# Two neighbouring rows on the partitions: six products in place of nine in the attention layer's output convolution

## The chip, the cores and the metric

The program runs on one core of one Trainium2 chip. TensorE does the matrix products into PSUM, VectorE (DVE) empties PSUM and does elementwise work and statistics, ScalarE (ACT) applies scale and bias, GpSimd (POOL) clears borders and copies, and SyncE's queue (SPq) issues nearly all the transfers, which run on 16 DMA engines. The metric is the time of one whole execution on the device, in microseconds. The kernel before takes 13737.34 us (median of 3 runs, 13731.92 to 13746.49).

## The reference, cut to what matters

Four layers, each `x = x + layer(group_norm(x))`, on four images of 48 channels and 256 x 256 pixels. The change concerns the first, an attention over channels:

```python
def _L0_conv_ref(x, qkv_w, dw_w, proj_w, temperature):
    qkv = conv1x1(x, qkv_w)                      # 48 -> 144 channels
    qkv = depthwise_conv3x3(qkv, dw_w)           # zero border
    q, k, v = split(qkv)                         # 48 channels each, over all 65536 pixels
    attn = softmax(einsum('bhcn,bhdn->bhcd', l2norm(q), l2norm(k)) * temperature)   # 48 x 48
    out = einsum('bhcd,bhdn->bhcn', attn, v)
    return conv1x1(out, proj_w)

x = x + _L0_conv_ref(_gn(x), ...)    # _gn: 16 groups of 3 channels, eps 1e-5
x = x + _L1_conv_ref(_gn(x), ...)    # next layer: needs the statistics of the new x
...
```

Once `attn` is known, projection, attention and the 1x1 convolution for `v` are three matrices on the channels of one image. Together with the depthwise 3x3 they make one 3x3 convolution of 48 to 48 channels whose weights differ from image to image.

## The kernel before: the parts that the change touches

`B, C, H, W = 4, 48, 256, 256`, `P = 96`, `R = 16` rows in a block, `NB = 16` blocks, `NP = 2` pairs of images. The 96 partitions hold two images of 48 channels each. First a pass over `x` gives the group norm's scale and bias for a pair (`coef[pair]`). Then for each pair: the products of q and k over all rows (`pqk`, `gram`), the softmax, the weights `wy`, and the output convolution (`py`), which reads `x` again.

```python
def ahead(items, load, work):            # loads of item i+1 stand before the work of item i
    ...

# layer 0: one block of 16 rows and its two neighbours, of both images of a pair
def load(pair, b):
    lo, hi = (1 if b == 0 else 0), (R + 1 if b == NB - 1 else R + 2)
    raw = raws.tile([P, R + 2, W], F32, tag="raw")                   # bufs=3
    src = x[rows(pair), (b * R - 1 + lo) * W : (b * R - 1 + hi) * W]
    nc.sync.dma_start(raw[:, lo:hi, :].rearrange(...), src)          # 18 KB in one piece per partition
    xn = big.tile([P, R + 2, W + 2], F32, tag="xn")                  # bufs=2
    nc.gpsimd.memset(...)                                            # borders
    nc.scalar.activation(xn[:, lo:hi, 1 : W + 1], raw[:, lo:hi, :], AF.Identity,
                         bias=coef[pair][:, 1:2], scale=coef[pair][:, 0:1])
    return raw, xn

# ... pqk and gram for all blocks, softmax, then pa = attention and projection of both images
wy = work.tile([P, 9, P], F32, tag="wy")
for t in range(9):
    wt = wv_sb * dwv_sb[:, t]                              # tensor_scalar_mul
    nc.tensor.matmul(pw, lhsT=wt, rhs=pa, start=True, stop=True)
    nc.vector.tensor_copy(wy[:, t, :], pw)                 # two 48 x 48 blocks, the rest zero

def outputs(b, loaded):
    raw, xn = loaded
    y = big.tile([P, R, W], F32, tag="y")
    for c in range(8):                                     # two rows of 256 in one PSUM bank
        ps = p_conv.tile([P, 2, W], F32, tag="pc", name="py")          # bufs=4
        for t, dy, dx in taps:                             # nine products
            nc.tensor.matmul(ps, lhsT=wy[:, t, :],
                             rhs=xn[:, 2 * c + dy : 2 * c + dy + 2, dx : dx + W],
                             start=t == 0, stop=t == 8)
        part = y[:, 2 * c : 2 * c + 2, :]
        nc.vector.tensor_add(part, ps, raw[:, 1 + 2 * c : 3 + 2 * c, :])
        nc.vector.bn_stats(stats[:, b * 8 + c, :], part)
    nc.sync.dma_start(x1[rows(pair), ...], y)              # 16 KB in one piece per partition

ahead(range(NB), lambda b: load(pair, b), outputs)
nc.vector.bn_aggr(mv, stats)
k.group_norm(work, p_small, mv, "mean3", coef1[pair])
```

The next layer starts with transfers of `x1` into tiles `tok`, which POOL copies into `pairs`, TensorE turns round (`ptok`) and DVE scales (`xt`) with `strip`, made from `coef1`.

Of the kernel before, what the change touches and what calls it, by code (L numbers as in the profile page):

```python
# [9 lines left out]
F32 = mybir.dt.float32  # L10
# [8 lines left out]
NP = 2  # L19
# [13 lines left out]
def _constants():  # L33
    i = np.arange(128)
    p = np.arange(P)
    group = lambda x: (x % C) // 3
    parts = {
        "ident": np.eye(128),

        "mean3": np.pad((p[:, None] // 3 == p[None] // 3) / 3.0, ((0, 32), (0, 0))),  # L40
        "mean6": np.pad((group(p)[:, None] == group(p)[None]) / 6.0, ((0, 32), (0, 0))),
        "mean8": (i[:, None] // F == i[None] // F) / float(F),
        "ones": np.ones((128, P)),

        "half": np.pad((p[:, None] // C == np.arange(2)[None]).astype(float), ((0, 32), (0, 0))),
        "diag48": np.pad((p[:, None] % C == np.arange(C)[None]).astype(float), ((0, 32), (0, 0))),

        "to_strip": np.pad(
            ((p[:, None] % 3 == 0) & (group(p)[:, None] % 2 == p[None] // C)).astype(float), ((0, 32), (0, 0))
        ),  # L50
        "of_strip": np.pad(
            (
                (p[:, None, None] // C == np.arange(2)[None, :, None])
                & (group(p)[:, None, None] // 2 == np.arange(G // 2)[None, None])
            ).reshape(P, G).astype(float),
            ((0, 32), (0, 0)),
        ),
    }
# [52 lines left out]
def rows(pair):  # L111
    return slice(pair * P, (pair + 1) * P)


@with_exitstack
def input_stats(ctx, tc, x, k, coef):

    nc = tc.nc
    big = ctx.enter_context(tc.tile_pool(name="s_big", bufs=4))
    work = ctx.enter_context(tc.tile_pool(name="s_work", bufs=2))  # L120
    psum = ctx.enter_context(tc.tile_pool(name="s_psum", bufs=2, space=PSUM))
    n = R * W

    def load(it):
        pair, b = it
        t = big.tile([P, n], F32, tag="x", name="sx")
        nc.sync.dma_start(t, x[rows(pair), b * n : (b + 1) * n])
        return t

    stats = [work.tile([P, NB * 8, 6], F32, tag="st", name=f"st{p}") for p in range(NP)]  # L130

    def add(it, t):
        pair, b = it
        for c in range(8):
            nc.vector.bn_stats(stats[pair][:, b * 8 + c, :], t[:, c * 512 : (c + 1) * 512])
        if b == NB - 1:
            mv = work.tile([P, 2], F32, tag="mv", name="mv")
            nc.vector.bn_aggr(mv, stats[pair].rearrange("p a b -> p (a b)"))
            k.group_norm(work, psum, mv, "mean3", coef[pair])

    ahead([(p, b) for p in range(NP) for b in range(NB)], load, add)


@with_exitstack
def layer0(ctx, tc, x, x1, wqk, dwqk, wv, dwv, projT, temp, k, coef, coef1):
# [18 lines left out]
    nc.sync.dma_start(wqk_sb, wqk)  # L164
    dw_sb = wp.tile([P, 9, NQ], F32, tag="dwqk", name="dw_sb")
    nc.gpsimd.dma_start(dw_sb.rearrange("p t o -> p (t o)"), dwqk.rearrange("t o -> (t o)").partition_broadcast(P))
    wq = wp.tile([P, 9, NQ], F32, tag="wq", name="wq")
    for t in range(9):
        nc.vector.tensor_mul(wq[:, t, :], dw_sb[:, t, :], wqk_sb)
# [9 lines left out]
    def load(pair, b):  # L179

        lo, hi = (1 if b == 0 else 0), (R + 1 if b == NB - 1 else R + 2)
        raw = raws.tile([P, R + 2, W], F32, tag="raw", name="raw")
        src = x[rows(pair), (b * R - 1 + lo) * W : (b * R - 1 + hi) * W]
        nc.sync.dma_start(raw[:, lo:hi, :].rearrange("p h w -> p (h w)"), src)
        xn = big.tile([P, R + 2, W + 2], F32, tag="xn", name="xn")
        nc.gpsimd.memset(xn[:, :, 0:1], 0.0)
        nc.gpsimd.memset(xn[:, :, W + 1 : W + 2], 0.0)
        if lo:
            nc.gpsimd.memset(xn[:, 0, :], 0.0)
        if hi < R + 2:  # L190
            nc.gpsimd.memset(xn[:, R + 1, :], 0.0)
        nc.scalar.activation(  # L192
            xn[:, lo:hi, 1 : W + 1], raw[:, lo:hi, :], AF.Identity, bias=coef[pair][:, 1:2], scale=coef[pair][:, 0:1]
        )
        return raw, xn

    taps = [(t, t // 3, t % 3) for t in range(9)]
    for pair in range(NP):
# [8 lines left out]
        pending = []  # L207

        def products(it, loaded):
            xn = loaded[1]  # L210
            for r in range(R):
                ps = p_conv.tile([128, 2, NQ], F32, tag="pc", name="pqk")
                for j in range(2):
                    for t, dy, dx in taps:
                        nc.tensor.matmul(  # L215
                            ps[:, j, :],
                            lhsT=xn[:, r + dy, dx + 128 * j : dx + 128 * j + 128],
                            rhs=wq[:, t, :],
                            start=t == 0,
                            stop=t == 8,  # L220
                        )
                qk = qkp.tile([128, 2, NQ], F32, tag="qk", name="qk")
# [18 lines left out]
            nc.tensor.matmul(pr, lhsT=k["ones", P], rhs=dg, start=True, stop=True)  # L241
            rsum.append(pr)
        norm = work.tile([P, P], F32, tag="norm", name="norm")
        half = k["half", P]
        nc.vector.tensor_scalar_mul(norm, rsum[0], half[:, 0:1])
        nc.vector.scalar_tensor_tensor(norm, rsum[1], half[:, 1:2], norm, ALU.mult, ALU.add)
        nc.vector.tensor_scalar_max(norm, norm, 1e-24)
# [24 lines left out]
        nc.tensor.matmul(pt, lhsT=attn.rearrange("p b d -> p (b d)"), rhs=proj_sb, start=True, stop=True)  # L272
        pa = work.tile([P, P], F32, tag="pa", name="pa")
        nc.vector.tensor_copy(pa, pt)
        wy = work.tile([P, 9, P], F32, tag="wy", name="wy")
        for t in range(9):
            wt = work.tile([P, P], F32, tag="wt", name="wt")
            nc.vector.tensor_scalar_mul(wt, wv_sb, dwv_sb[:, t : t + 1])
            pw = p_small.tile([P, P], F32, tag="small", name="pw")
            nc.tensor.matmul(pw, lhsT=wt, rhs=pa, start=True, stop=True)  # L280
            nc.vector.tensor_copy(wy[:, t, :], pw)

        stats = work.tile([P, NB * 8, 6], F32, tag="st", name="st")

        def outputs(b, loaded):
            raw, xn = loaded
            y = big.tile([P, R, W], F32, tag="y", name="y")
            for c in range(8):
                ps = p_conv.tile([P, 2, W], F32, tag="pc", name="py")
                for t, dy, dx in taps:  # L290
                    nc.tensor.matmul(  # L291
                        ps,
                        lhsT=wy[:, t, :],
                        rhs=xn[:, 2 * c + dy : 2 * c + dy + 2, dx : dx + W],
                        start=t == 0,
                        stop=t == 8,
                    )
                part = y[:, 2 * c : 2 * c + 2, :]
                nc.vector.tensor_add(part, ps, raw[:, 1 + 2 * c : 3 + 2 * c, :])  # L299
                nc.vector.bn_stats(stats[:, b * 8 + c, :], part.rearrange("p h w -> p (h w)"))  # L300
            nc.sync.dma_start(x1[rows(pair), b * R * W : (b + 1) * R * W], y.rearrange("p h w -> p (h w)"))

        ahead(range(NB), lambda b: load(pair, b), outputs)
        mv = work.tile([P, 2], F32, tag="mv", name="mv")
        nc.vector.bn_aggr(mv, stats.rearrange("p a b -> p (a b)"))
        k.group_norm(work, p_small, mv, "mean3", coef1[pair])


@with_exitstack
def layer1(ctx, tc, x1, x2, w1, w2, pw, cols, b2, k, coef1, coef2):  # L310
# [34 lines left out]

    strip = []
    for b in range(B):
        of = k["of_strip", P][:, (b % 2) * NS : (b % 2 + 1) * NS]
        one = wp.tile([P, 2, NS], F32, tag=f"strip{b}", name=f"strip{b}")
        for c in range(2):  # L350
            spread = work.tile([P, NS], F32, tag="spread", name="spread")
            nc.vector.tensor_scalar_mul(spread, of, coef1[b // 2][:, c : c + 1])
            ps = p_small.tile([P, NS], F32, tag="small", name="pstrip")
            nc.tensor.matmul(ps, lhsT=k["to_strip", P], rhs=spread, start=True, stop=True)
            nc.vector.tensor_copy(one[:, c, :], ps)
        strip.append(one)
# [474 lines left out]
def program(ctx, tc, a, out, at):  # L831
# [5 lines left out]
    coefs = [  # L837
        [const.tile([P, 2], F32, tag=f"coef{layer}_{p}", name=f"coef{layer}_{p}") for p in range(NP if layer < 2 else B)]
        for layer in range(4)
    ]  # L840
    x1 = dram.tile([B * C, HW], F32, tag="x1", name="x1")
# [19 lines left out]
def _layout(v):  # L861
# [4 lines left out]
    dw = v["L0_conv_dw_w"].reshape(3 * C, 9)  # L866
    a["wqk"] = _block_diag(qkv[: 2 * C].T, 2)
    a["dwqk"] = np.concatenate([dw[: 2 * C].T] * 2, 1)
    a["wv"] = _block_diag(qkv[2 * C :], 2)
# [63 lines left out]
```

## Time and profile before

| stretch of the span, us | what runs | TensorE busy, us |
|---|---|---|
| 0 to 240 | statistics of x | 4.16 |
| 240 to 1926 | pqk and gram, images 0 and 1 | 1681.05 |
| 1943 to 2928 | py, images 0 and 1 | 985.00 |
| 2935 to 4612 | pqk and gram, images 2 and 3 | 1677.00 |
| 4631 to 5617 | py, images 2 and 3 | 986.00 |
| 5617 to 7400 | second layer | 1273.20 |
| 7400 to 13280 | third and fourth layer | 5446.95 |
| 13280 to 13735 | output put in order | 0.00 |

How to read it: a stretch in which TensorE is busy from end to end gets shorter only if TensorE has less to do there; in the others something else ends the waits. "PE" is TensorE's products and "PEld" its weight loads, which go on beside the products. In this profile a product of 32-bit numbers appears as two instructions, so 2304 products of the output convolution are counted as x4608.

### The profile page before, as it was taken

Reading aid. Unit: us, or ns where it says so; the run is one execution under the profiler, and the core shown is the slowest. Engines: PE = TensorE matmul, PEld = TensorE weight load, DVE = VectorE, ACT = ScalarE, POOL = GpSimd, SP = SyncE. Lnnn points to the kernel's source line nnn. Section 1 sums busy time; section 2 is a strip of 40 time slices with the busy share of each in tenths; the row PEclk is TensorE's granted clock in tenths of the full one; section 3 lists DMA queues with packets and bytes.
Section 4 is the critical chain, followed back from the end, with each engine's and each line's share of the span. In section 5 each row is a group of like instructions: output and inputs, shape, how many; then the busy total and the mean of one; then the engine's idle time right before and its main releaser. Section 6 shows DMA issues by size and latency. Waiting matters only on the chain.

```text
span 13735.6 us, 130672 instructions
## 1 busy us (share of the span) xinstructions
PE 12080.9 (88%) x55056; PEld 8710.1 (63%) x55056; DVE 4075.2 (30%) x6994; ACT 3100.0 (23%) x4523; POOL 755.4 (5%) x367
## 2 busy tenths in 40 slices
PE   2999999999999999877866989899888989899960
PEld 2999973369999633333323767676665767676740
DVE  5000011110000111444543323354553323354530
ACT  0000000000000000111112533254444533354531
POOL 0000000000000000100100000000331000001430
PEclk9999999999999999988987999999998999999985
DMA  7000002110000021243326756664775756655889
GB/s 176 22 16 16 16 16 59 51 52 16 16 21 16 20 59 49 77 97 86 77 56 129 154 119 149 152 164 132 186 183 116 154 126 147 157 150 147 228 195 226
DMA packets 867508, 1383.31 MB, mean 101 GB/s; under 512 B 245064, under 2 KB 791016, under 8 KB 791560
## 3 DMA queue, kind: packets, MB, share of 16 engines
q1 hardware_dynamic: 866776, 1374.29, 42.1%
q8 instruction: 431, 7.06, 0.2%
q14 instruction: 157, 1.29, 0.0%
q0 software_dynamic: 144, 0.66, 0.0%
HBM read 820.20 MB, written 553.65 MB: 100 GB/s over the span
## 4 chain that ended last, share of the span: by engine, by line
PE 81%; SPq 5%; DMA 4%; issue 4%; DVE 3%; POOL 1%; ACT 1%; POOLq 0%; ACTq 0%; DVEq 0%
PE ps L564 35%; PE pqk L215 22%; PE py L291 14%; PE ph L386 3%; SPq L809 3%; PE gram L205 3%; PE psp L444 2%; DMA sx<-in_x 1%; SPq L504 1%; DMA xr<-x 1%; POOL sl L767 1%; PE pout L483 1%; DVE v L423 1%; PE ptok L391 1%; SPq L649 0%
## 5 line engine op out<-in xcount | busy, mean ns | idle before, releaser
L564 PE MATMUL ps<-carry,w_sb 96*96 96x256 f32 x24480 | 5443.1, 384 | 394.8 <-DVE carry L720 129.1
L564 PEld LDWEIGHTS ps<-carry,w_sb 96*96 96x96 f32 x24480 | 4030.8, 165 | 1806.4 <-DVE carry L566 170.2
L215 PE MATMUL pqk<-wq,xn 96*128 96x192 f32 x18432 | 3101.9, 327 | 12.4 <-ACT xn L192 10.9
L215 PEld LDWEIGHTS pqk<-wq,xn 96*128 96x128 f32 x18432 | 2991.4, 190 | 13.5 <-ACT xn L192 11.4
L291 PE MATMUL py<-xn,wy 96*96 96x512 f32 x4608 | 1985.3, 593 | 0.2
L568 DVE SCALAR_TENSOR_TENSOR carry<-ps,b_sb,col 96x256 f32<-96x256 f32 x2040 | 1359.6, 667 | 1247.0 <-PE ps L564 1215.6
L722 ACT COPY col<-carry 96x256 f32<-96x256 f32 x2040 | 1333.9, 654 | 1627.8 <-DVE carry L568 1627.8
L291 PEld LDWEIGHTS py<-xn,wy 96*96 96x96 f32 x4608 | 749.8, 163 | 1223.8 <-issue 1223.3
L192 ACT ACTIVATE xn<-raw,coef 96x4608 f32<-96x4608 f32 (+1 forms) x64 | 269.1, 4204 | 4990.0 <-PE pqk L215 3223.3
L223 DVE COPY qk<-pqk 128x384 f32<-128x384 f32 x512 | 285.5, 558 | 3083.0 <-PE pqk L215 3083.0
L767 POOL TENSOR_TENSOR sl<-sl,col 96x4096 f32<-96x4096 f32 x64 | 567.6, 8888 | 5314.3 <-ACT col L722 4514.6
L566 DVE TENSOR_TENSOR carry<-ps,up 96x256 f32<-96x256 f32 x1016 | 426.4, 421 | 1020.0 <-PE ps L564 921.1
L566 DVE TENSOR_TENSOR carry<-ps,dn 96x256 f32<-96x256 f32 x1020 | 427.7, 421 | 1000.0 <-PE ps L564 945.7
L299 DVE TENSOR_TENSOR y<-py,raw 96x512 f32<-96x512 f32 x256 | 175.8, 687 | 1611.6 <-PE py L291 1611.6
L623 ACT ACTIVATE dn<-carry,b_sb 96x256 f32<-96x256 f32 x1024 | 499.5, 504 | 660.8 <-DVE carry L566 660.5
L663 ACT COPY up<-carry 96x256 f32<-96x256 f32 x1016 | 410.0, 404 | 945.5 <-DVE carry L566 944.8
L483 PE MATMUL pout<-h,w_sb 128*96 128x512 f32 x512 | 341.0, 816 | 297.0 <-DVE y L491 296.2
L386 PE MATMUL ph<-xt,w_sb 96*128 96x512 f32 x1024 | 499.1, 608 | 103.7 <-DVE xt L393 81.1
L205 PE MATMUL gram<-qk 128*96 128x96 f32 x4096 | 431.3, 248 | 0.0
L483 PEld LDWEIGHTS pout<-h,w_sb 128*96 128x96 f32 x512 | 100.6, 216 | 520.9 <-issue 495.6
L205 PEld LDWEIGHTS gram<-qk 128*96 128x96 f32 x4096 | 428.6, 164 | 0.3
L393 DVE TENSOR_SCALAR xt<-ptok,strip 96x512 f32<-96x512 f32 x256 | 298.8, 1195 | 241.5 <-PE ptok L391 239.8
(108 smaller groups left out, 2950.4 us busy)
## 6 DMA issues: line engine op xcount, KB each, us to landing
dn<-x SPq DMA_DIRECT2D x256, 384.0 KB, 11.4
D<-dn SPq DMA_DIRECT2D x32, 3072.0 KB, 21.5
up<-D SPq DMA_DIRECT2D x32, 3072.0 KB, 28.2
col<-U SPq DMA_DIRECT2D x64, 1536.0 KB, 13.7
sl<-x SPq DMA_DIRECT2D x64, 1536.0 KB, 16.5
R<-col SPq DMA_DIRECT2D x64, 1536.0 KB, 11.7
col<-R SPq DMA_DIRECT2D x64, 1536.0 KB, 25.6
x<-sl SPq DMA_DIRECT2D x64, 1536.0 KB, 7.2
```

The costliest lines, as they stand in the source:

```text
L205: nc.tensor.matmul(grams[b], lhsT=part, rhs=part, start=first and j == 0, stop=last and j == 1)
L215: nc.tensor.matmul(ps[:, j, :], lhsT=xn[:, r + dy, dx + 128 * j : dx + 128 * j + 128], rhs=wq[:, t, :], start=t == 0, stop=t == 8,)
L291: nc.tensor.matmul(ps, lhsT=wy[:, t, :], rhs=xn[:, 2 * c + dy : 2 * c + dy + 2, dx : dx + W], start=t == 0, stop=t == 8,)
L386: nc.tensor.matmul(ph[f], lhsT=w1_sb[:, i, f, :], rhs=xt, start=i == 0, stop=i == NS - 1)
L483: nc.tensor.matmul(ps.rearrange("p h w -> p (h w)"), lhsT=w2_sb[:, i, :], rhs=h1[:, p0 : p0 + 512], start=True, stop=True,)
L564: nc.tensor.matmul(ps, lhsT=w_sb[:, way, j, :], rhs=old[:, :, j : j + W // 2], start=j == 0, stop=j == 2)
L566: nc.vector.tensor_add(blocks(new), blocks(ps), inp)
L568: nc.vector.scalar_tensor_tensor(new, ps, b_sb[:, way : way + 1], inp, ALU.add, ALU.add)
L623: nc.scalar.activation(inp, new, AF.Identity, bias=b_sb[:, 0:1])
L722: nc.scalar.copy(column, step(pair, way, column, False))
L767: nc.gpsimd.tensor_add(v, v, flat(got[pair]))
L809: nc.sync.dma_start(t[b * C : (b + 1) * C, r].rearrange("c k q h w -> c (k q) (h w)"), xin[r * C : (r + 1) * C, 2 * pair + b, :, n * NH : ...
```

## The change

The output convolution goes image by image. The 96 partitions hold the 48 channels of one image twice: an odd row below and the even row after it above (row -1 with row 0, row 1 with row 2, and so on). The outputs are rows 2m and 2m+1. They need the four rows 2m-1 to 2m+2, which are two such row pairs, so that two positions of the pair by three columns, six products, cover the 3x3 window of both output rows, where one row per partition needed nine. Each 96 x 96 weight matrix has three of its four 48 x 48 blocks filled. The aim is fewer products on TensorE for the same outputs.

With it come these: the rows are read and written with a step of two (pieces of 1 KB); the even rows are read once more for the residual, because `xn`'s order no longer matches the output's; the scale and bias are needed per image with both halves of the partitions alike, so the first pass over `x` goes per image, its two halves of the rows on the two halves of the partitions; the q and k products still go by pairs and put their scale and bias together from two images.

```diff
 # first pass: one image, upper and lower half of its rows on the two halves of the partitions
+        for half in range(2):
+            p0 = half * HW // 2 + i * n
+            nc.sync.dma_start(t[half * C : (half + 1) * C], x[b * C : (b + 1) * C, p0 : p0 + n])
-            k.group_norm(work, psum, mv, "mean3", coef[pair])
+            k.group_norm(work, psum, mv, "mean6", coef[b])
 ...
+    M = R // 2
+    def load_odd(b, n, edges):
+        t = big.tile([P, M + 1, W], F32, tag="odd", name="odd")          # bufs=2, like all of big
+        ...
+        for r in range(2):
+            lo, hi = ...
+            h0 = n * R - 1 + r
+            nc.sync.dma_start(t[r * C : (r + 1) * C, lo:hi, :], src[:, h0 + 2 * lo : h0 + 2 * hi - 1 : 2, :])
+        even = big.tile([P, M, W], F32, tag="even", name="even")
+        for r in range(2):
+            nc.sync.dma_start(even[r * C : (r + 1) * C], src[:, n * R + r : n * R + r + R - 1 : 2, :])
+        xn = big.tile([P, M + 1, W + 2], F32, tag="xodd", name="xodd")
+        nc.gpsimd.memset(...)                                            # borders
+        nc.scalar.activation(xn[:, lo:hi, 1 : W + 1], t[:, lo:hi, :], AF.Identity, bias=g[:, 1:2], scale=g[:, 0:1])
+        if edge is not None:                                             # first and last block: the row outside is zero
+            nc.scalar.activation(xn[:, edge, 1 : W + 1], t[:, edge, :], ...)
+        return xn, even
 ...
-            nc.vector.tensor_copy(wy[:, t, :], pw)
+            nc.vector.tensor_copy(py[:, t, :], pw)
+        for b in (2 * pair, 2 * pair + 1):
+            wy = work.tile([P, 2, 3, 2, C], F32, tag="wy", name="wy")
+            ...                                                          # six DVE instructions fill it from py
+            def outputs(n, loaded):
+                xn, even = loaded
+                y = big.tile([P, M, W], F32, tag="y", name="y")
+                for c in range(M // 2):
+                    ps = p_conv.tile([P, 2, W], F32, tag="pc", name="py")
+                    for i in range(6):
+                        j, dx = i // 3, i % 3
+                        nc.tensor.matmul(ps, lhsT=wy[:, j, dx].rearrange("p r o -> p (r o)"),
+                                         rhs=xn[:, 2 * c + j : 2 * c + j + 2, dx : dx + W],
+                                         start=i == 0, stop=i == 5)
+                    part = y[:, 2 * c : 2 * c + 2, :]
+                    nc.vector.tensor_add(part, ps, even[:, 2 * c : 2 * c + 2, :])
+                    nc.vector.bn_stats(stats[:, n * 4 + c, :], part.rearrange("p h w -> p (h w)"))
+                for r in range(2):
+                    nc.sync.dma_start(dst[:, n * R + r : n * R + r + R - 1 : 2, :], y[r * C : (r + 1) * C])
+            ahead(range(NB), lambda n: load_odd(b, n, edges), outputs)
+            ...
+            k.group_norm(work, p_small, mv, "mean6", coef1[b])
```

More of the change, by code (lines that the diff above doesn't have):

```diff
@@ L38, in _constants @@
         "ident": np.eye(128),
-        "mean3": np.pad((p[:, None] // 3 == p[None] // 3) / 3.0, ((0, 32), (0, 0))),
         "mean6": np.pad((group(p)[:, None] == group(p)[None]) / 6.0, ((0, 32), (0, 0))),
@@ L122, in input_stats @@
     n = R * W
+    nb = NB // 2
     def load(it):
-        pair, b = it
+        b, i = it
         t = big.tile([P, n], F32, tag="x", name="sx")
-        nc.sync.dma_start(t, x[rows(pair), b * n : (b + 1) * n])
+        for half in range(2):
+            p0 = half * HW // 2 + i * n
+            nc.sync.dma_start(t[half * C : (half + 1) * C], x[b * C : (b + 1) * C, p0 : p0 + n])
         return t
-    stats = [work.tile([P, NB * 8, 6], F32, tag="st", name=f"st{p}") for p in range(NP)]
+    stats = [work.tile([P, nb * 8, 6], F32, tag="st", name=f"st{b}", bufs=B) for b in range(B)]
     def add(it, t):
-        pair, b = it
+        b, i = it
         for c in range(8):
-            nc.vector.bn_stats(stats[pair][:, b * 8 + c, :], t[:, c * 512 : (c + 1) * 512])
-        if b == NB - 1:
+            nc.vector.bn_stats(stats[b][:, i * 8 + c, :], t[:, c * 512 : (c + 1) * 512])
+        if i == nb - 1:
             mv = work.tile([P, 2], F32, tag="mv", name="mv")
-            nc.vector.bn_aggr(mv, stats[pair].rearrange("p a b -> p (a b)"))
-            k.group_norm(work, psum, mv, "mean3", coef[pair])
-    ahead([(p, b) for p in range(NP) for b in range(NB)], load, add)
+            nc.vector.bn_aggr(mv, stats[b].rearrange("p a b -> p (a b)"))
+            k.group_norm(work, psum, mv, "mean6", coef[b])
+    ahead([(b, i) for b in range(B) for i in range(nb)], load, add)
 @with_exitstack
@@ L166, in layer0 @@
     nc.gpsimd.dma_start(dw_sb.rearrange("p t o -> p (t o)"), dwqk.rearrange("t o -> (t o)").partition_broadcast(P))
+    half = k["half", P]
+    pairs = []
+    for pair in range(NP):
+        both = wp.tile([P, 2], F32, tag=f"both{pair}", name=f"both{pair}")
+        nc.vector.tensor_scalar_mul(both, coef[2 * pair], half[:, 0:1])
+        nc.vector.scalar_tensor_tensor(both, coef[2 * pair + 1], half[:, 1:2], both, ALU.mult, ALU.add)
+        pairs.append(both)
     wq = wp.tile([P, 9, NQ], F32, tag="wq", name="wq")
@@ L192, in load @@
         nc.scalar.activation(
-            xn[:, lo:hi, 1 : W + 1], raw[:, lo:hi, :], AF.Identity, bias=coef[pair][:, 1:2], scale=coef[pair][:, 0:1]
+            xn[:, lo:hi, 1 : W + 1], raw[:, lo:hi, :], AF.Identity, bias=pairs[pair][:, 1:2], scale=pairs[pair][:, 0:1]
         )
-        return raw, xn
+        return xn
+    M = R // 2
+    def load_odd(b, n, edges):
+        t = big.tile([P, M + 1, W], F32, tag="odd", name="odd")
+        src = x[b * C : (b + 1) * C, :].rearrange("c (h w) -> c h w", w=W)
+        edge = 0 if n == 0 else M if n == NB - 1 else None
+        if edge is not None:
+            nc.gpsimd.memset(t[:, edge, :], 0.0)
+        for r in range(2):
+            lo, hi = (1 if edge == 0 and r == 0 else 0), (M if edge == M and r == 1 else M + 1)
+            h0 = n * R - 1 + r
[4 more added lines that the diff above has]
+        xn = big.tile([P, M + 1, W + 2], F32, tag="xodd", name="xodd")
+        nc.gpsimd.memset(xn[:, :, 0:1], 0.0)
+        nc.gpsimd.memset(xn[:, :, W + 1 : W + 2], 0.0)
+        g = coef[b]
+        lo, hi = (1 if edge == 0 else 0), (M if edge == M else M + 1)
+        nc.scalar.activation(
+            xn[:, lo:hi, 1 : W + 1], t[:, lo:hi, :], AF.Identity, bias=g[:, 1:2], scale=g[:, 0:1]
+        )
+        if edge is not None:
+            g = edges[edge == M]
+            nc.scalar.activation(
+                xn[:, edge, 1 : W + 1], t[:, edge, :], AF.Identity, bias=g[:, 1:2], scale=g[:, 0:1]
+            )
+        return xn, even
     taps = [(t, t // 3, t % 3) for t in range(9)]
@@ L209, in products @@
         def products(it, loaded):
-            xn = loaded[1]
+            xn = loaded
             for r in range(R):
@@ L243, in layer0 @@
         norm = work.tile([P, P], F32, tag="norm", name="norm")
-        half = k["half", P]
         nc.vector.tensor_scalar_mul(norm, rsum[0], half[:, 0:1])
@@ L274, in layer0 @@
         nc.vector.tensor_copy(pa, pt)
-        wy = work.tile([P, 9, P], F32, tag="wy", name="wy")
+        py = work.tile([P, 9, P], F32, tag="py", name="py")
         for t in range(9):
@@ L280, in layer0 @@
             nc.tensor.matmul(pw, lhsT=wt, rhs=pa, start=True, stop=True)
-            nc.vector.tensor_copy(wy[:, t, :], pw)
[L283 to L306, printed above, removed]
+            nc.vector.tensor_copy(py[:, t, :], pw)
+        for b in (2 * pair, 2 * pair + 1):
+            wy = work.tile([P, 2, 3, 2, C], F32, tag="wy", name="wy")
+            tap = lambda dy: py[:, 3 * dy : 3 * dy + 3, (b % 2) * C : (b % 2 + 1) * C]
+            nc.vector.tensor_scalar_mul(wy[:, 0, :, 0, :], tap(0), half[:, 0:1])
+            nc.vector.scalar_tensor_tensor(wy[:, 0, :, 0, :], tap(1), half[:, 1:2], wy[:, 0, :, 0, :], ALU.mult, ALU.add)
+            nc.vector.tensor_scalar_mul(wy[:, 0, :, 1, :], tap(0), half[:, 1:2])
+            nc.vector.tensor_scalar_mul(wy[:, 1, :, 0, :], tap(2), half[:, 0:1])
+            nc.vector.tensor_scalar_mul(wy[:, 1, :, 1, :], tap(1), half[:, 0:1])
+            nc.vector.scalar_tensor_tensor(wy[:, 1, :, 1, :], tap(2), half[:, 1:2], wy[:, 1, :, 1, :], ALU.mult, ALU.add)
+            edges = []
+            for r in (1, 0):
+                e = work.tile([P, 2], F32, tag=f"edge{r}", name=f"edge{r}")
+                nc.vector.tensor_scalar_mul(e, coef[b], half[:, r : r + 1])
+                edges.append(e)
+            stats = work.tile([P, NB * 4, 6], F32, tag="st", name="st")
+            def outputs(n, loaded):
[5 more added lines that the diff above has]
+                        j, dx = i // 3, i % 3
+                        nc.tensor.matmul(
+                            ps,
+                            lhsT=wy[:, j, dx].rearrange("p r o -> p (r o)"),
+                            rhs=xn[:, 2 * c + j : 2 * c + j + 2, dx : dx + W],
+                            start=i == 0,
+                            stop=i == 5,
+                        )
+                    part = y[:, 2 * c : 2 * c + 2, :]
+                    nc.vector.tensor_add(part, ps, even[:, 2 * c : 2 * c + 2, :])
+                    nc.vector.bn_stats(stats[:, n * 4 + c, :], part.rearrange("p h w -> p (h w)"))
+                dst = x1[b * C : (b + 1) * C, :].rearrange("c (h w) -> c h w", w=W)
+                for r in range(2):
+                    nc.sync.dma_start(dst[:, n * R + r : n * R + r + R - 1 : 2, :], y[r * C : (r + 1) * C])
+            ahead(range(NB), lambda n: load_odd(b, n, edges), outputs)
+            mv = work.tile([P, 2], F32, tag="mv", name="mv")
+            nc.vector.bn_aggr(mv, stats.rearrange("p a b -> p (a b)"))
+            k.group_norm(work, p_small, mv, "mean6", coef1[b])
@@ L347, in layer1 @@
     for b in range(B):
-        of = k["of_strip", P][:, (b % 2) * NS : (b % 2 + 1) * NS]
+        of = k["of_strip", P][:, :NS]
         one = wp.tile([P, 2, NS], F32, tag=f"strip{b}", name=f"strip{b}")
@@ L351, in layer1 @@
             spread = work.tile([P, NS], F32, tag="spread", name="spread")
-            nc.vector.tensor_scalar_mul(spread, of, coef1[b // 2][:, c : c + 1])
+            nc.vector.tensor_scalar_mul(spread, of, coef1[b][:, c : c + 1])
             ps = p_small.tile([P, NS], F32, tag="small", name="pstrip")
@@ L837, in program @@
     coefs = [
-        [const.tile([P, 2], F32, tag=f"coef{layer}_{p}", name=f"coef{layer}_{p}") for p in range(NP if layer < 2 else B)]
+        [const.tile([P, 2], F32, tag=f"coef{layer}_{b}", name=f"coef{layer}_{b}") for b in range(B)]
         for layer in range(4)
@@ L868, in _layout @@
     a["dwqk"] = np.concatenate([dw[: 2 * C].T] * 2, 1)
-    a["wv"] = _block_diag(qkv[2 * C :], 2)
+    a["wv"] = np.tile(qkv[2 * C :], (2, 2))
     a["dwv"] = np.concatenate([dw[2 * C :]] * 2, 0)
```

## The prediction, made before the changed kernel ran

> **What bounds the kernel now.** I read the busy shares first, then the chain of work that ended last, then the table of stretches for the two places where the changed line runs. On the page, TensorE is busy for 88% of the span and makes up 81% of the chain; line 291, the output convolution, is 14% of the chain.
>
> ```profile
> PE 12080.9 (88%) x55056; PEld 8710.1 (63%) x55056; DVE 4075.2 (30%) x6994; ACT 3100.0 (23%) x4523; POOL 755.4 (5%) x367
> ...
> L291 PE MATMUL py<-xn,wy 96*96 96x512 f32 x4608 | 1985.3, 593 | 0.2
> L291 PEld LDWEIGHTS py<-xn,wy 96*96 96x96 f32 x4608 | 749.8, 163 | 1223.8 <-issue 1223.3
> ...
> L299 DVE TENSOR_TENSOR y<-py,raw 96x512 f32<-96x512 f32 x256 | 175.8, 687 | 1611.6 <-PE py L291 1611.6
> ```
>
> An average over the span does not say what holds in this stage, so I took the chain in order of time (start, length, what) and then the busy times by stretch (length; PE, PEld, DVE, ACT, POOL; granted clock, DMA share, GB/s):
>
> ```profile
> 1943.07 985.49 PE py L291 x2296
> ...
> 4631.67 985.49 PE py L291 x2296
> ```
>
> ```profile
> 1943.00:2928.00 985.00, 985.00 (x2297) 373.15 (x2296) 175.35 (x256) 63.05 (x15) 3.22 (x32) 1.00 0.18 53
> 4631.00:5617.00 986.00, 986.00 (x2299) 373.42 (x2298) 175.15 (x255) 60.30 (x15) 2.73 (x29) 1.00 0.16 48
> 1926.50:1943.00 16.50, 10.04 (x35) 5.51 (x34) 7.97 (x36) 4.77 (x4) 0.00 (x0) 0.69 0.01 2
> 5617.00:5641.00 24.00, 5.82 (x25) 4.74 (x25) 9.83 (x32) 0.26 (x1) 2.87 (x2) 0.58 0.91 249
> 13280.00:13735.00 455.00, 0.00 (x0) 0.00 (x0) 37.76 (x32) 62.41 (x32) 0.00 (x0) 0.50 1.05 224
> ```
>
> The reader is to see that both stages are one unbroken run of products at full clock: 2296 instructions in 985.49 us, one every 429.2 ns. The 593 ns of the group line is one instruction's own length, which overlaps its neighbours; the price of one more or one fewer is the 429.2. Weight loads (163 ns) fit beside them. DVE is busy for 175 of 985 us, ACT for 63, the DMA engines for 18%. A third less TensorE work shortens this stage until one of these takes over. Three rows serve later: the setup of the weights (1926.5 to 1943), the hand-over to the second layer (5617 to 5641), and the last stretch, which is transfers alone.
>
> [...]
>
> **The change part by part.**
>
> (1) Products. Before: 2 pairs x 16 blocks x 8 groups x 9 = 2304, each of 512 columns. After: 4 images x 16 blocks x 4 groups x 6 = 1536, also of 512 columns. The order of instructions in the built kernel has the same number, 768 to a pair. 768 products fewer x 2 instructions x 429.2 ns = **-659.3 us**, all of it on the path.
>
> (2) What stands beside the products. A block (16 rows of one image) takes 24 x 858.4 ns = 20.6 us of TensorE. DVE: four adds of 0.69 us and four bn_stats of 0.69 us = 5.5 us. The count over the stage is 256 of each as before, because a group still fills 96 x 512. ACT: the old activation took 4.23 us for 4608 elements a partition, so 2304 take some 2.1 us. Bytes: 48 channels x (18 + 16) rows x 1 KB read and 48 x 16 x 1 KB written, 2.46 MB, or 119 GB/s over 20.6 us, where the stage had 53. The last stretch moves 224 GB/s, and half of that is pieces of 512 B:
>
> ```profile
> oi<-x SPq DMA_DIRECT2D x64, 768.0 KB, 17.5
> ...
> x<-y SPq DMA_DIRECT2D x128, 384.0 KB, 7.0
> ```
>
> The 768 KB are 48 x 32 pieces of 512 B, the 384 KB are 48 x 32 pieces of 256 B. So 1 KB pieces should carry at least 200 GB/s, and the DMA engines would be some 55% busy. SyncE's queue issues six transfers a block, of 384 or 432 pieces. In the second layer four issues of 1536 pieces each take this long:
>
> ```profile
> 6003.95 7.23 SPq L504 DMA_DIRECT2D x<-y  x4
> ```
>
> That is 1.8 us for one, so six cost at most 11 us, probably 3. All of this fits in 20.6 us: **0**. In the built order the odd rows of block n+3 are asked for once block n+2 is normalised, right after block n's products; that leaves more than a block's time for their landing. Even rows of n+2 are asked for at the end of block n and needed at the end of the first group of n+2, 25.7 us later; 1.7 MB landed in 14.6 us before. The loads of image 1 also stand in the queue before the last blocks of image 0, so between images of a pair there is no gap for a load.
>
> (3) Weights. Before, the nine `pw` products were woven between the first products of `py`; in the built order all nine stand first, and six DVE instructions on 96 x 144 elements (some 0.3 us each) follow. From `pa` at 1934 us I count nine rounds of 0.6 us and 1.8 us of DVE, so `py` starts at about 1941.5 with nothing done. Before, at 1942.9 five products (4.3 us) were done. The loss is some 3 us a pair: **+6**.
>
> (4) Ends of images. TensorE meets the group norm's small products three products after an image's end; the chain of add, bn_stats and bn_aggr (half of 3.62 us now) takes 3.3 us against 2.6 us of products, then four small DVE steps. About 2 us of waiting, at two more places: **+4**. The aggregation at the end of pair 0 and of the first pass is shorter by 1.8 us each: **-3**.
>
> (5) Hand-over to the second layer. Before, the `tok` loads were issued after the last store, and `ptok` began at 5640.2, 23 us after the last `py`. In the built order the first four `tok` loads and their POOL copies stand before the output stage of pair 1, whose buffers are smaller, so the space is free. `ptok` can follow `py` at once; the first `xt` then waits for the group norm, some 7 us after the last `py` against 24. **-17**.
>
> Sum: -659.3 + 0 + 6 + 4 - 3 - 17 = -669, so 13737 - 669 = **13068 us**.
>
> **The rivals.** *Transfers become the bound.* For it: twice the rate, 1 KB pieces, two half-partition transfers for each tile[...]. Against it: 224 GB/s with pieces of 512 B. If 1 KB pieces with a step carried only 100 GB/s, a block would take 24.6 us in place of 20.6; 64 blocks x 4 us = 256 us of the gain lost, 13325 us. *The issue queue or a buffer becomes the bound.* [...]the odd loads wait for ACT, so a late activation would hold back the next stores and loads. The sign would be gaps at each block's start. With 2 us a block it costs 128 us: 13195 us. I see nothing in the built order that makes it so. *The clock falls.* The weight matrices are three quarters full instead of half, and the granted clock was 1.00 here; the scan layers, with fuller matrices, show 0.94, but with 7% of TensorE's time idle. A clock of 0.94 over 1318 us would cost 84 us: 13150 us. *The first pass or the second layer shifts* by 10 us either way through split loads and another order.
>
> **Range and chances.** The main term is a count times a measured pace, so most of the doubt lies in small terms and in rivals that can only lose. The range is 13035 to 13130: below, 33 us for a luckier second layer; above, 60 us for the clock or a small wait at each block. Chances: faster by over 2% (under 13463 us) 0.96, within 2% 0.03, slower by over 2% 0.01. Even the transfer rival at 100 GB/s leaves more than 2%.
>
> **What would show it.** Right: `py` as x3072 with about 1320 us busy, two runs of about 659 us on the chain, no idle time before `py` but at images' ends; DMA near 119 GB/s and a share of about 0.5 there; `ptok` under 10 us after the last `py`; the other stretches as long as before. Wrong: idle time before `py` ended by ACT or DMA, a pace other than 429 ns, or a first pass longer than 231 us.

## The result, and the profile after

The changed kernel takes 13125.88 us (median of 4 runs, 13119.12 to 13128.02) against 13741.01 us before (median of 4 on the same chips): a ratio of 0.9552, 95% interval 0.9536 to 0.9569. It is 615 us faster. The prediction was 13068 us with a range of 13035 to 13130, so the range held, just, and the prediction was 58 us too low.

The changed stage on the page of the kernel after (busy us, mean ns of one, idle time before):

```profile
PE 11437.6 (87%) x53536; PEld 8465.5 (64%) x53536; DVE 4087.8 (31%) x7058; ACT 3117.3 (24%) x4567; POOL 759.9 (6%) x435
...
L350 PE MATMUL py<-xodd,wy 96*96 96x512 f32 x3072 | 1324.7, 594 | 1.3 <-DVE wy L331 1.3
...
L358 DVE TENSOR_TENSOR y<-py,even 96x512 f32<-96x512 f32 x256 | 175.9, 687 | 949.5 <-PE py L350 949.5
```

The count is 3072, the busy time 1985.3 - 1324.7 = 660.6 us less, and TensorE waited 1.3 us before these products in all. The chain in order of time shows two runs for each pair, one for each image (start, length, what):

```profile
1990.51 331.74 PE py L350 x768
2327.13 326.32 PE py L350 x760
4347.05 332.76 PE py L350 x768
4684.70 326.32 PE py L350 x760
```

326.32 / 760 = 429.4 ns an instruction, where it was 429.2 before: the same pace. The stretches of these stages (length; PE, PEld, DVE, ACT, POOL; granted clock, DMA share, GB/s):

```profile
1990.50:2653.50 663.00, 662.14 (x1542) 250.78 (x1543) 180.69 (x276) 74.28 (x37) 5.78 (x66) 1.00 0.58 115
4347.00:5011.30 664.30, 663.10 (x1540) 250.63 (x1540) 181.78 (x280) 71.71 (x35) 5.47 (x63) 1.00 0.56 111
```

The clock stayed at 1.00 with the fuller weight matrices, and the transfers, twice as dense as before (111 to 115 GB/s for 48 to 53), fill 0.56 to 0.58 of the DMA engines. The hand-over to the second layer, from the timelines (TensorE only), first of the kernel before, where the last `py` ended at 5617, then of the kernel after, where it ended at 5011:

```profile
5640.19 1.94 PE L391 MATMUL ptok<-cst,pairs 128*96 128x128 f32 x8 [10.08 <-POOL pairs L367]
```

```profile
5011.78 1.08 PE L452 MATMUL ptok<-cst,pairs 128*96 128x128 f32 x8 [0.78 <-DVE y L358]
...
5019.83 2.08 PE L447 MATMUL ph<-xt,w_sb 96*128 96x512 f32 x2 [0.72 <-DVE strip L416]
```

All this is near what was predicted. The loss shows where the prediction had put almost nothing, in the first pass over `x`. The first load of layer 0 (`raw`) is issued when the first pass is over; the kernel before, then after (durations in ns, then first and last start in us):

```profile
L184 SPq DMA_DIRECT2D raw<-in_x x64: 312/313/2357, 231.0 to 5432.9; - x64
```

```profile
L194 SPq DMA_DIRECT2D raw<-in_x x32: 312/312/427, 282.3 to 3812.5; - x32
```

The same 190 us of the first pass, before and then after, in the columns of the stretches above:

```profile
10.00:200.00 190.00, 0.96 (x4) 0.79 (x4) 139.64 (x231) 1.54 (x2) 0.00 (x0) 1.00 1.00 235
```

```profile
10.00:200.00 190.00, 1.88 (x8) 1.57 (x8) 112.67 (x194) 1.80 (x3) 0.00 (x0) 1.00 1.01 185
```

The DMA engines are busy all the time in both, but move 185 GB/s in place of 235. The whole difference of the two profiled runs, between points that both traces have:

| from, to | before, us | after, us | difference |
|---|---|---|---|
| start, first `raw` issued | 231.0 | 282.3 | +51.3 |
| first `raw`, first `ph` of the second layer | 5411.6 | 4737.5 | -674.1 |
| first `ph`, first `dn` load | 1747.1 | 1753.9 | +6.8 |
| first `dn` load, first `oi` load | 5895.1 | 5902.8 | +7.7 |
| first `oi` load, end | 450.8 | 449.7 | -1.1 |
| sum | 13735.6 | 13126.2 | -609.4 |

The two small positive rows are not put down to the change. In the runs below that leave these stages and the places of their tiles alone, the third row was 1744 to 1749 us and the fourth 5894 to 5904 us; three of them are forms of the changed kernel (1745.1, 1746.6 and 1749.4 us), so the 1753.9 us belong to this one execution.

### The profile page after: what moved, and what is told of

It reads as the page before. It is cut to its first block, busy times and chain, and to the rows that moved or that the text cites. A ratio compares the mean times of both kernels' runs of the same rounds, so it can differ in the third digit from the quotient of the medians.

```text
span 13126.2 us, 128482 instructions
## 1 busy us (share of the span) xinstructions
PE 11437.6 (87%) x53536; PEld 8465.5 (64%) x53536; DVE 4087.8 (31%) x7058; ACT 3117.3 (24%) x4567; POOL 759.9 (6%) x435
## 4 chain that ended last, share of the span: by engine, by line
PE 80%; SPq 6%; DMA 5%; issue 4%; DVE 3%; POOL 1%; ACT 1%; POOLq 0%; ACTq 0%; DVEq 0%
PE ps L625 37%; PE pqk L257 23%; PE py L350 10%; PE ph L447 3%; SPq L870 3%; PE gram L247 3%; PE psp L505 2%; DMA sx<-in_x 2%; SPq L565 1%; DMA xr<-x 1%; POOL sl L828 1%; PE pout L544 1%; DVE v L484 1%; PE ptok L452 1%; DMA col<-R 1%
## 5 line engine op out<-in xcount | busy, mean ns | idle before, releaser
L350 PE MATMUL py<-xodd,wy 96*96 96x512 f32 x3072 | 1324.7, 594 | 1.3 <-DVE wy L331 1.3
L350 PEld LDWEIGHTS py<-xodd,wy 96*96 96x96 f32 x3072 | 500.4, 163 | 821.1 <-issue 819.3
L202 ACT ACTIVATE xn<-raw,both 96x4608 f32<-96x4608 f32 (+1 forms) x32 | 134.5, 4204 | 2993.6 <-PE pqk L257 2878.9
L358 DVE TENSOR_TENSOR y<-py,even 96x512 f32<-96x512 f32 x256 | 175.9, 687 | 949.5 <-PE py L350 949.5
L229 ACT ACTIVATE xodd<-odd,coef 96x2304 f32<-96x2304 f32 (+1 forms) x64 | 146.2, 2284 | 1189.9 <-PE py L350 1048.4
```

The source lines that it names most:

```text
L350: nc.tensor.matmul(ps, lhsT=wy[:, j, dx].rearrange("p r o -> p (r o)"), rhs=xn[:, 2 * c + j : 2 * c + j + 2, dx : dx + W], start=i == 0, s ...
```

## The experiments

**The changed kernel with the old first pass.** One transfer of 96 partitions for a tile, two images at a time, group norm by pairs, then the coefficients of each image copied to both halves of the partitions:

```diff
-        for half in range(2):
-            p0 = half * HW // 2 + i * n
-            nc.sync.dma_start(t[half * C : (half + 1) * C], x[b * C : (b + 1) * C, p0 : p0 + n])
+        nc.sync.dma_start(t, x[rows(pair), b * n : (b + 1) * n])
 ...
+            k.group_norm(work, psum, mv, "mean3", both[pair])
+            for h in range(2):                      # "dup": a new 96 x 192 constant of zeros and ones
+                nc.tensor.matmul(pd, lhsT=k["dup", P][:, h * P : (h + 1) * P], rhs=both[pair], ...)
+                nc.vector.tensor_copy(coef[2 * pair + h], pd)
```

> The changed kernel with the first pass over x as it was before: one transfer of 96 partitions (two images) for a tile, and the scale and bias of each image then copied to both halves of the partitions by four small products. Theory A (the missing 52 us of the prediction are in the first pass, because of its split loads): the last load's issue goes from 282 us back to about 231 us and the whole time falls by 50 us, to about 13075 us. Rival (the loss comes from the new bookkeeping of scale and bias per image, or from later layers): the whole time stays at 13126 us, within 10.

Measured: 13006.96 us (12996.73 to 13012.56), ratio to before 0.9465, interval 0.9452 to 0.9478. The first `raw` is issued at 235.4 us, so theory A holds for the first pass. But the whole is 119 us shorter than the kernel after, not 50. The rest lies in stages that this edit doesn't touch: the second layer from `ph` to `dn` took 1712.2 us in place of 1753.9, and the output stretch was some 30 us shorter. That called for a second theory, tried further down.

**Four ways to split the first pass of the kernel before.** All read the same bytes from the same addresses into the same tiles; only the split differs, and in b_spread the partition in which a row lands. These four runs, the next one and the run with nine products are single executions. The same first pass ended at 282.3 us in the kernel after and at 277.4 us in the run with nine products, so a difference of some 5 us says nothing.

```diff
-        nc.sync.dma_start(t, x[rows(pair), b * n : (b + 1) * n])
 # b_halves
+        for s in range(2):
+            nc.sync.dma_start(t[s * C : (s + 1) * C], x[pair * P + s * C : ..., b * n : (b + 1) * n])
 # b_cols
+        for s in range(2):
+            nc.sync.dma_start(t[:, s * (n // 2) : (s + 1) * (n // 2)], x[rows(pair), p0 : p0 + n // 2])
 # b_spread: rows of b_halves, into every second partition
+            nc.sync.dma_start(t[s::2, :], x[pair * P + s * C : ..., b * n : (b + 1) * n])
 # b_thirds
+        for s in range(3):
+            nc.sync.dma_start(t[s * 32 : (s + 1) * 32], x[pair * P + s * 32 : ..., b * n : (b + 1) * n])
```

> The kernel before, with each tile of the first pass brought by two transfers, one for each half of the partitions (0 to 47 and 48 to 95), from the same addresses as before; nothing else changed. If half-partition transfers are what is slow, or the doubled number of transfers: the first raw load is issued near 282 us in place of 231, whole time 13790 us. If it is the addresses in memory (upper and lower half of one image side by side, which this kernel does not read): it stays at 231 us, whole time 13740 us.

Measured: first `raw` at 293.1 us, whole time 13803.28 us. The kernel before gets the whole loss, and more, from this edit alone; the addresses in memory were not needed for it.

> The kernel before, with each tile of the first pass brought by two transfers of all 96 partitions, each with half of the columns (pieces of 8 KB); as many transfers of the same 768 KB as in the changed kernel. If the number or the size of the transfers is what is slow: first raw load near 282 us. If it is how many partitions a transfer covers, or the addresses: it stays near 231 us.

Measured: first `raw` at 213.2 us, 13724.12 us. As many transfers of the same size are not slow: they are 18 us faster than one large one. Neither number nor size of the transfers is the cause.

> The kernel before, with each tile of the first pass brought by two transfers of 48 rows, the first into the even partitions and the second into the odd ones, so that each covers the whole width of 96 partitions with 48 pieces of 16 KB; the group statistics then mix the wrong channels, the work is the same. If it is the narrow band of 48 neighbouring partitions that is slow: the first raw load is issued near 231 us again. If it is the number of 48 rows to a transfer, whichever partitions they land in: near 282 us.

Measured: first `raw` at 226.6 us, 13732.82 us. With 48 rows of 16 KB to a transfer, as in b_halves, but spread over 96 partitions, the loss is gone. Which partitions a transfer reaches is what decides here. Three such stretches, of b_halves, b_cols and b_spread in this order:

```profile
10.00:200.00 190.00, 0.96 (x4) 0.79 (x4) 108.08 (x179) 1.54 (x2) 0.00 (x0) 1.00 1.01 180
```

```profile
10.00:200.00 190.00, 0.96 (x4) 0.79 (x4) 152.68 (x249) 1.54 (x2) 0.00 (x0) 1.00 1.02 253
```

```profile
10.00:200.00 190.00, 0.96 (x4) 0.79 (x4) 141.74 (x235) 1.54 (x2) 0.00 (x0) 1.00 1.01 239
```

The reader is to see the last column, 180, 253 and 239 GB/s, with the engines busy for 1.01 to 1.02 of the time in each: a full DMA share does not say how much is moved.

> The kernel before, with each tile of the first pass brought by three transfers of 32 neighbouring partitions each, from the same addresses. If the narrow band of partitions is what slows the first pass (48 wide: 293 us against 231 at 96), 32 wide is slower still: the first raw load is issued at 320 us or later. If the halves were slow for another reason (a seam at partition 48, two transfers in place of one): near 293 us or below.

Measured: first `raw` at 248.7 us, 13759.14 us. The simple form, "the narrower the slower", falls: 32 partitions do better than 48.

```profile
10.00:200.00 190.00, 0.96 (x4) 0.79 (x4) 130.25 (x215) 1.54 (x2) 0.00 (x0) 1.00 1.01 216
```

**Two transfers of 64 and 32 partitions,** again in the kernel before:

```diff
+        for lo, hi in ((0, 64), (64, P)):
+            nc.sync.dma_start(t[lo:hi], x[pair * P + lo : pair * P + hi, b * n : (b + 1) * n])
```

> The kernel before, with each tile of the first pass brought by two transfers of 64 and 32 partitions (0 to 63, 64 to 95), from the same addresses. Three bands of 32 did better (249 us) than two of 48 (293 us), so width alone does not rank them. [...]

Measured: first `raw` at 248.4 us, 13751.18 us, 216 GB/s like the three bands of 32.

```profile
10.00:200.00 190.00, 0.95 (x4) 0.79 (x4) 130.12 (x215) 1.54 (x2) 0.00 (x0) 1.00 1.01 216
```

The runs on the kernel before agree in this: bands of neighbours are slower (180 to 216 GB/s) than the full width (235) or a spread (239). Width alone does not rank them: three bands of 32, and one of 64 with one of 32, moved 216 GB/s, two of 48 moved 180; that is the further 45 us between 248 and 293. Nothing here separates the two bands of 48, or the band of 64 from that of 32. So the loss follows from the band, and why 48 neighbours are slower than 32 or 64 is not shown.

**The same spread in the changed kernel:**

```diff
-            nc.sync.dma_start(t[half * C : (half + 1) * C], x[b * C : (b + 1) * C, p0 : p0 + n])
+            nc.sync.dma_start(t[half::2, :], x[b * C : (b + 1) * C, p0 : p0 + n])
```

> The changed kernel with one edit: in the first pass the upper half of an image's rows lands in the even partitions and the lower half in the odd ones, in place of 0 to 47 and 48 to 95. Number, size and addresses in memory of the transfers are those of the changed kernel; the statistics then mix the wrong channels. If the band of partitions is the cause of the longer first pass: the first raw load at 230 us in place of 282, whole time 13074 us. If it is reading two halves of an image side by side: still 282 us, 13126 us.

Measured: first `raw` at 212.7 us, 13049.95 us (13042.18 to 13058.00), ratio to before 0.9501, interval 0.9485 to 0.9517. The scale and bias belong to wrong channels here, the work is the same. One edit of the destination takes 70 us off the first pass and 76 us off the whole, more than the loss. So the band is the cause in the changed kernel too, and reading the two halves of an image side by side costs nothing that shows. Why it gets faster than the old first pass (212.7 against 231.0 us) was not tried. The first pass of the kernel after_spread:

```profile
10.00:200.00 190.00, 2.81 (x12) 2.36 (x12) 155.66 (x269) 2.06 (x4) 0.00 (x0) 1.00 1.01 254
```

**Where the tiles begin.** The old first pass brought a larger table of constants, which moved every later tile. In the built programs the tiles `sx` of the first pass, `xr` and `y` of the second layer and `oi` and `oo` of the output stretch begin 64 bytes behind a multiple of 256 in the kernels before and after, and at a multiple of 256 in the changed kernel with the old first pass. (The expectations below say "every stage"; most of the other tiles begin at other distances in all three kernels.) Three runs move them by an unused tile and nothing else, after_pad from the kernel after, before_pad from the kernel before and pair_off64 from pairpass, the changed kernel with the old first pass:

```diff
+    pad = const.tile([128, n], F32, tag="pad", name="pad")   # n = 48 in after_pad and before_pad, 16 in pair_off64
+    nc.gpsimd.memset(pad, 0.0)
```

> The changed kernel with one unused tile of 192 bytes behind the constants, so that the big tiles of every stage begin at a multiple of 256 bytes in their partition instead of 64 bytes behind one. Theory B (the 70 us by which the kernel with the old first pass beat its expectation come from where its larger table of constants happened to put the tiles): the second layer shrinks by some 40 us, the output stretch by some 30 us, the whole time to about 13056 us; the first pass keeps its length of 282 us. Rival (they come from the old first pass itself, or from the size of the table in memory): the time stays at 13126 us.

Measured: 13041.69 us (13028.27 to 13050.71), ratio 0.9494, interval 0.9480 to 0.9508. The second layer, `ph` to `dn`, took 1706.4 us. The first pass got shorter as well, 264.2 us, which was not expected:

```profile
10.00:200.00 190.00, 1.88 (x8) 1.57 (x8) 122.67 (x211) 1.80 (x3) 0.00 (x0) 1.00 1.01 201
```

> The kernel before with the same unused tile of 192 bytes: its tiles begin at a multiple of 512 bytes instead of 64 bytes behind a multiple of 256. Theory B: about 13670 us, the same two stages 70 us shorter. Rival: 13740 us.

Measured: 13671.56 us (13665.30 to 13673.42), ratio 0.9954, interval 0.9937 to 0.9970. The second layer took 1711.0 us in place of 1747.1, the output stretch 419.3 in place of 450.8.

> The changed kernel with the old first pass, and one unused tile of 64 bytes behind the constants, which puts its tiles 64 bytes behind a multiple of 256 again, as in the kernels before and after. Theory B: the 70 us are lost again, about 13077 us, second layer near 1754 us and output stretch near 405 us; this is then the price of the first pass alone against the changed kernel's 13126. Rival: 13007 us.

Measured: 13071.26 us (13065.89 to 13072.49), ratio 0.9516, interval 0.9501 to 0.9530; second layer 1746.6 us. Theory B holds in all three for the second layer and the output stretch. What it left out is the first pass: the band of 48 costs 51 us where the tiles begin 64 bytes behind a multiple of 256 (282.3 us against 231.8 in pair_off64), and 29 us where they begin at one (264.2 against 235.4 in pairpass). The whole times say nearly the same: 54.6 and 34.7 us. With transfers of all 96 partitions the place made no clear difference to the first pass (231.8 and 235.4 us; 231.0 before and 226.9 in before_pad). Middle of the output stretch, of the kernels pairpass and pair_off64, which differ by 64 bytes:

```profile
12588.00:12971.00 383.00, 0.00 (x0) 0.00 (x0) 35.40 (x30) 58.68 (x30) 0.00 (x0) 0.50 1.07 242
```

```profile
12616.00:13031.00 415.00, 0.00 (x0) 0.00 (x0) 35.40 (x30) 58.48 (x30) 0.00 (x0) 0.50 1.08 223
```

Same work, same counts, 383 against 415 us. In the second layer the time in which SyncE's queue issues stores of 256 byte pieces shows it too. Three groups of four such stores took 5.88 to 5.98 us in pairpass, and 7.35 to 8.02 us in the kernel after; one group of four, pairpass and then pair_off64:

```profile
5340.20 5.98 SPq L564 DMA_DIRECT2D x<-y  x4
```

```profile
5335.44 7.63 SPq L564 DMA_DIRECT2D x<-y  x4
```

What makes the place count is not shown: the unused tile moves all the later tiles at once, and only two places of the tiles named above were measured, 64 bytes behind a multiple of 256 and at one.

**Nine products again,** in the changed kernel:

```diff
-                    for i in range(6):
-                        j, dx = i // 3, i % 3
+                    for i in range(9):
+                        j, dx = i // 3 % 2, i % 3        # the first row pair's three are added twice
 ...
-                            stop=i == 5,
+                            stop=i == 8,
```

> The changed kernel with nine products to a group again (the three of the first row pair are added a second time, so the outputs are other numbers; transfers, vector work and buffers are those of the changed kernel). If the gain is the count of products at 429 ns an instruction: 768 products more cost 659 us, 13785 us, slower than the kernel before by the 50 us of the first pass. If the shorter stage came from elsewhere (fewer bytes in a block, order, hand-over): clearly less, under 13700 us.

Measured: 13773.30 us. The outputs are other numbers, transfers and vector work are the same. From the start of the first `py` to that of the last it takes 5664.9 - 1986.3 = 3678.6 us, against 5010.4 - 1990.5 = 3019.9 us in the kernel after: 658.7 us for 768 products. Its chain in the first pair:

```profile
1986.33 496.79 PE py L350 x1152
2488.01 491.12 PE py L350 x1144
```

With the old count the rest of the change loses: 13773.30 is 39 us slower than the kernel before (13734.75 beside this run).

**The version for use.** The old first pass by pairs, its tiles brought by two transfers of half the columns and placed at a multiple of 256, as in pairpass:

```diff
 # pairpass
-        nc.sync.dma_start(t, x[rows(pair), b * n : (b + 1) * n])
+        for s in range(2):
+            p0 = b * n + s * (n // 2)
+            nc.sync.dma_start(t[:, s * (n // 2) : (s + 1) * (n // 2)], x[rows(pair), p0 : p0 + n // 2])
```

> The version for use: the changed kernel with the old first pass by pairs, tiles at a multiple of 256 bytes, and each tile of the first pass brought by two transfers of all 96 partitions, half the columns each, which took 18 us off the first pass of the kernel before. Expected 12990 us, first raw load at about 215 us; if the 18 us do not add to the gain from the tiles' places: 13007 us.

Measured: 12978.83 us (12974.84 to 12988.66), ratio to before 0.9450, interval 0.9437 to 0.9463; first `raw` at 207.8 us, 28 us before that of pairpass. The whole is 147 us less than the kernel after.

## Why the prediction was right, and where it was off

(1) Products: -659.3 us predicted. 660.6 us by the busy time, and 658.7 us when only the count was put back. The pace stayed at 429 ns.

(2) What stands beside them: 0 predicted, and TensorE waited 1.3 us for anything before `py`. The rates came out at 111 to 115 GB/s for 119 and a DMA share of 0.56 to 0.58 for 0.55. The transfers of 1 KB pieces fill more of the engines for what they move (0.58 at 115 GB/s, 0.18 at 53 before) and are still hidden. They are also bands of 48 partitions, and the residual's loads bring all sixteen rows of a block again, not only the even ones; both are hidden behind the products. SyncE's queue took some 5.2 us for the six issues of a block (0.85 + 3.29 + 1.03 us in the one from 2013.93), where 3 to 11 were expected and a block has 20.6. The granted clock was 1.00. The rivals of transfers, issue queue and clock all fell in this stage.

(3) Weights: +3 us a pair predicted. From the end of the last gram product to the first `py` it takes 1990.51 - 1977.01 = 13.5 us in the first pair of the kernel after. Before, the same way to steady products was 16.3 us, and on it stood four products, not the five that the prediction counted (two instructions each):

```profile
1935.27 1.99 PE L291 MATMUL py<-xn,wy 96*96 96x512 f32 x2
...
1937.70 1.91 PE L291 MATMUL py<-xn,wy 96*96 96x512 f32 x2
...
1940.05 1.66 PE L291 MATMUL py<-xn,wy 96*96 96x512 f32 x2
...
1941.88 1.02 PE L291 MATMUL py<-xn,wy 96*96 96x512 f32 x2
...
1942.91 4.89 PE L291 MATMUL py<-xn,wy 96*96 96x512 f32 x11
```

Less their 3.4 us that is 12.8 us, so the loss is 0.7 us. In the second pair the same count gives 12.8 us after and 13.9 before, so the two pairs together lose nothing where 6 us were predicted. The prediction's estimates for the parts were near: five `pw` rounds in 2.96 us, 0.59 each for 0.6, and 0.30 to 0.36 us for each of the six DVE instructions, for 0.3.

(4) Ends of images: at the two added places TensorE waited 0.85 and 0.84 us before the group norm's product, where 2 us each were allowed; at the end of the first pair, an old place, 1.15 us in place of 2.56. (The "-3" is two times 1.8 us, so -3.6.) (5) Hand-over: from the last `py` to the first `ph` 8.8 us, 25.4 us before: -16.6, predicted -17. All rows from the first `raw` to the first `ph` together: -674.1 measured, about -668 predicted.

The term that was mis-sized is in the first pass. The prediction let it fall by half of its "-3"; that two transfers to two halves of the partitions lose little beside one was the author's estimate, which no trace had shown. It was +51.3 us, and that is nearly the whole miss of 58. The place to look was known: "a first pass longer than 231 us" stood under what would make it wrong, and as a rival of "10 us either way". No term asked what rate a transfer to 48 neighbouring partitions has, though the whole pass is bound by its loads (DMA share 1.00 in the kernel before). The one rate that the prediction used for transfers to half of the partitions, 224 GB/s in the last stretch, was a mixture of loads of 48 partitions and stores of 96.

That the range held is partly luck. Its upper 60 us were meant for the clock or a small wait at each block, neither of which came; the first pass, which was allowed 10 us, used them up. Nor did the prediction look at where tiles begin. Those named above kept their distance of 64 bytes by chance, and the 192 unused bytes of after_pad alone are worth 84 us, more than the miss.

The run pair_off64 is the kernel that the prediction had priced: six products, a first pass as before, tiles in the old place. It took 13071.26 us, 663 us less than the kernel before beside it, where -669 was predicted.

## What to carry to other kernels

Where one engine is busy from end to end, price a change by its pace (the time from one start to the next) and the count (here 429.2 ns and 1536 instructions, 659.3 us priced and 660.6 measured); then go through every stage that the change touches for its own bound, the short ones too. Price a transfer-bound stage by which partitions each transfer reaches and where its tiles begin, not by bytes and a rate from another shape: here the same bytes of the first pass moved at 180 to 255 GB/s. Before comparing two versions to a per cent, see where their tiles begin: here 64 bytes were worth 64 us (pairpass against pair_off64), more than the 55 us of the first pass that was under study.

## What the runs showed of the hardware that was not expected

- Loads of 48 neighbouring partitions moved 180 to 185 GB/s, and 201 where the tiles began at a multiple of 256 bytes; bands of 32 or of 64 and 32 moved 216, all 96 at once 230 to 235, 48 rows in every second partition 239 to 254, with a DMA share of 1.00 to 1.01 in each.
- Two transfers of half the columns for a tile beat one of all: 253 against 235 GB/s, 18 us of 231 (and 255 against 230 GB/s, 28 us of 235, with the tiles at a multiple of 256 bytes).
- Tiles that begin at a multiple of 256 bytes, against 64 bytes behind one: the second layer 1706 to 1712 us in place of 1744 to 1754, the output stretch 241 to 242 GB/s in place of 223 to 224. The kernel before gains 0.46% from 192 unused bytes.
